# First-stage stores moved to GpSimd's queue, raw matrices loaded in thirds, and the statistics' roots unpinned, in a fused ConvNeXt block and gate

## The chip, the cores and the metric

The kernel runs on one core of a Trainium2 chip. The metric is the device time of one execution in microseconds (us). TensorE (PE) multiplies matrices and writes PSUM; VectorE (DVE), ScalarE (ACT) and GpSimd (POOL) do elementwise work; SyncE (SP) issues DMAs. Every engine works through its own instructions in order, and semaphores tie the engines together.

## The reference, cut to what matters

Thirty-two images of 384 channels, 28 x 28 pixels, go through a ConvNeXt block and then through a channel gate, all in float32:

```
y = depthwise_conv_7x7(x) + dw_b
y = (y - mean_c(y)) * rsqrt(var_c(y) + 1e-6) * ln_g + ln_b      # over channels, per pixel
y = gelu(y @ w1 + b1)                                           # 384 -> 1536
gx = sqrt(sum over pixels of y^2);  nx = gx / (mean_f(gx) + 1e-6)
y = grn_g * (y * nx) + grn_b + y
z = x + y @ w2 + b2                                             # 1536 -> 384
out = sigmoid(z + gate(mean, max, min of z over pixels))
```

## The kernel before

There are two parts. The **first stage** (lines 360 to 865) does the depthwise convolution of all images at once, channel by channel, as products on TensorE. The **image stage** (lines 869 to 1248) then takes the images one after the other: `up` (the product with w1), `down` (the product with w2), `gate_store`. Both matrix products are cut into block products with fewer multiplications (`UPSTEPS`, `STEPS`), which need sums of blocks of w1 and of w2. These sums (u1 and u2) are formed once, in the first stage, and kept in DRAM (`u1d`, `u2d`).

The first stage runs over 48 steps `s` of 8 channels each. A step has four pairs of channels. For a pair, `conv` (line 651) does six products into a PSUM tile `pc`; DVE transposes it into `yt` (line 682) and adds it to `acc` (line 690); ACT squares it into `sq` (line 696); after every second pair GpSimd adds `sq` to `ssum` (line 702). At the end of a step `yt` is stored to `yd` in DRAM (line 837). There are two `yt` buffers, two `sq` buffers and four `pc` buffers. Loads run ahead: the Toeplitz tables `tmat` (line 422) three steps, and the input planes (line 457) eight groups; a plane's buffer is free again when ACT has copied it into `xpad` (line 474), from where TensorE turns it (line 484) and DVE and ACT copy it into `xt` (lines 493, 495).

Between these lie the weights. `later` (line 633) says at which step a raw matrix or vector is loaded: w1 at step 2 and, into the same tile `ws`, w2 at step `U2 - 3` = 20. Ahead of each such load GpSimd writes one element of its target with a value of `acc` (line 788), so that the load waits for one engine only. `center_w` (line 561) folds the layer norm into w1 in steps 7 to 10: twelve groups of small products first, then twelve products into `pm`, and after every fourth of these three updates of w1 on DVE (line 597). `form_w` (line 543) makes one u tile: a first ACT or GpSimd instruction (lines 553, 550) and then one GpSimd addition for each further term (line 556). The fifteen u1 tiles are formed at the ends of steps 11 to 19, the thirty-eight u2 tiles at the ends of steps 23 to 44. All share three buffers of one tile (pool `ufp`). A finished tile is put into `stores` and stored by SP at the end of the next step (line 853).

The last two steps are done in two halves of sixteen images (line 802). Each half's `yt` is stored in quarters, by SP and ACT in turn (line 815). Then `finish` (line 711) makes the layer norm's statistics of a half on DVE, with a square root on ACT (line 730), and SP stores them (line 733) for the image stage, which reads them back as `rb` (line 289). `first_image` (line 748) prepares image 0 without the scale by its statistics, which `stretch` (line 904) multiplies in later. `normed` (line 308, operation on line 315) applies `rb` to the other images. In `up`, products go to PSUM banks `ph_A`, `ph_B`, `ph_C` (line 941), and each bank is evacuated by ACT copies (line 948) and DVE additions (lines 952 to 960).

What sets the order: the program is traced in the order of the code. The framework then places each instruction on its engine's list when its operands are ready, the earlier traced one first. `keep(...)`, or `tc.keep_in_program_order`, pins an instruction behind the one traced before it on its engine; without it an instruction may move ahead.

Of the kernel before, what the change touches and what calls it, by code (L numbers as in the profile page):

```python
# [23 lines left out]
EPS = 1e-6  # L24
# [9 lines left out]
TC = 8  # L34
# [12 lines left out]
SQ = 4  # L47
NQD = P // PW
# [40 lines left out]
KT = FB // 3  # L89
# [94 lines left out]
UD = 2  # L184
# [13 lines left out]
def convnext_gate_kernel(  # L198
# [109 lines left out]
    def normed(b, cbs=range(CB)):  # L308

        if b not in accs:  # L310
            accs[b] = (
                xp.tile([P, CB, NT], F32, tag="x", name=f"acc_{b}") if b == 1 else room_acc
            )
        for cb in cbs:
            nc.vector.scalar_tensor_tensor(  # L315
                accs[b][:, cb].rearrange("p (r w) -> p r w", w=HW), rows(yis[b][:, cb]),
                dwb_t[:, cb : cb + 1], rows(rbs[b]), ALU.add, ALU.mult,
            )

    def affine(eng, out, in_, mul, add):  # L320
        if eng is nc.vector:
# [38 lines left out]
    with ExitStack() as one:  # L360
# [78 lines left out]
        xi_last = tp.tile([P, NT], F32, name="xi_last")  # L439
        ssum = finp.tile([P, SQ, N], F32, name="ssum")  # L440
        acc = finp.tile([P, 2, N], F32, name="acc")
        fin = finp.tile([P, 3, N], F32, name="fin")
        dws = finp.tile([P, 1], F32, name="dws")
        lr = tp.tile([P, CB, 2], F32, name="lr")
        mcol = tp.tile([P, FB], F32, name="mcol")
        for t in (ssum, acc, fin[:, 0]):
            nc.gpsimd.memset(t, 0.0)
        GT = NX * NG
        xis = {}
# [15 lines left out]

        keep = tc.keep_in_program_order

        def pad_x(i):
            dst = xpad[i % NPAD][:, :, :HW]
            src = xis.pop(i).rearrange("p (r w) -> p r w", w=HW)  # L470
            if i < NG:
                nc.gpsimd.tensor_copy(dst, src)
            else:
                keep(nc.scalar.activation(dst, src, AF.Identity))

# [25 lines left out]
        w1r = ws.rearrange("p (k f) -> p k f", f=FF)  # L501
        w1v = ws.rearrange("p (k t m c) -> p t k m c", t=KT, m=3, c=P)
        w2v = ws.rearrange("p (t k m c) -> p t k m c", t=KD, k=4, c=P)
        U1, U2 = 11, 23
        stores = []
        SG = 20

# [32 lines left out]
                )  # L540


        def form_w(name, wv, text, dst):

            t = ufp.tile([P, KT, P], F32, tag="uf", name=name)[:, : wv.shape[1], :]
            todo = sorted(terms(text), key=lambda x: -x[0])
            blks = [(sg, wv[:, :, int(k), m, :]) for sg, m, k in todo]
            if len(blks) > 1 and blks[0][0] > 0:
                (_, a), (sg, c) = blks[:2]
                nc.gpsimd.tensor_tensor(t, a, c, ALU.add if sg > 0 else ALU.subtract)  # L550
                del blks[:2]
            else:
                keep(nc.scalar.activation(t, blks[0][1], AF.Identity, scale=float(blks[0][0])))
                del blks[:1]
            for sg, blk in blks:
                nc.gpsimd.tensor_tensor(t, t, blk, ALU.add if sg > 0 else ALU.subtract)
            stores.append((dst, t))

        cent = {}

# [43 lines left out]
        def pad_next(i):  # L604
            if i < GT:
                pad_x(i)
                if i + AHEAD < GT:
                    load_x(i + AHEAD)

        for i in range(AHEAD):  # L610
            load_x(i)
        xt = new_xt(0)
        for i in range(NG):
            pad_x(i)
            if i == 0:
                load_t(0, 2)
                nc.sync.dma_start(dwb, cvec[0:1, :].broadcast_to([P, C]))
            if i == NG - 2:
                for cb in range(CB):
                    if cb:  # L620
                        keep(sequences(cb))
                    keep(nc.scalar.dma_start(fs[cb][P:, :], zrow))
            if i == NG - 2:

                nc.gpsimd.tensor_copy(tmat[1][:, 0, :1], xpad[i % NPAD][:, 0, :1])
# [7 lines left out]
        later = {  # L633
            2: (
                ws.rearrange("p (cb f) -> p cb f", f=FF),
                w1.rearrange("(cb p) f -> p cb f", p=P),
            ),
            U2 - 3: (
                ws.rearrange("p (fb c) -> p fb c", c=C),
                w2.rearrange("(fb p) c -> p fb c", p=P),  # L640
            ),
            1: (cv, cvec.rearrange("v (cb p) -> p v cb", p=P)),
            4: (fv, fvec.rearrange("v (fb p) -> p v fb", p=P)),
            6: (awt[:, 0], aw[0].rearrange("(cb p) r -> p cb r", p=P)),
            7: (awt[:, 1], aw[1].rearrange("(cb p) r -> p cb r", p=P)),
            8: (w22b, w22.broadcast_to([P, R])),
# [61 lines left out]

        pcs = []

        def finish(half, b0, b1):

            def part(v):
                return v.rearrange("p (j b) -> p j b", b=B)[:, :, b0:b1]

            rs, s2 = (part(fin[:, i]) for i in range(2))
            mu, va = (part(acc[:, i]) for i in range(2))
            keep(nc.vector.tensor_tensor(mu, mu, va, ALU.add))
            keep(
                nc.vector.tensor_reduce(  # L720
                    s2,
                    ssum.rearrange("p c (j b) -> p j b c", b=B)[:, :, b0:b1],
                    AX.X, ALU.add,
                )
            )
            keep(nc.vector.tensor_scalar(mu, mu, dws, 1.0 / C, ALU.add, ALU.mult))
            keep(nc.vector.tensor_tensor(va, mu, mu, ALU.mult))
            keep(nc.vector.scalar_tensor_tensor(va, s2, 1.0 / C, va, ALU.mult, ALU.subtract))
            keep(nc.vector.tensor_scalar(va, va, 0.0, EPS, ALU.max, ALU.add))
            nc.scalar.activation(s2, va, AF.Sqrt)  # L730
# [44 lines left out]
        for s in range(NK):  # L775
            k, si = divmod(s, SK)
            if s + 3 < NK:
                if s == 0:
                    for i in range(2, 4):
                        nc.gpsimd.tensor_copy(tmat[i][:, 0, :1], xpad[i % NPAD][:, 0, :1])  # L780
                        if i == 2:
                            load_t(i)
                load_t(s + 3)
# [11 lines left out]
            if s == NK - 1:  # L795
# [6 lines left out]
                for half, (b0, b1) in enumerate(((0, B0), (B0, B))):  # L802
                    if b0 == b1:
                        continue
                    if half:
                        y2 = new_yt("yt_b0"), new_yt("yt_b1")
                        for i in range(0, NS, UG):
                            for t in range(2):
                                first_u1[t, i] = load_u1(t, i)
                    for n in range(2 * PAIRS):  # L810
                        i, c2 = divmod(n, PAIRS)
                        conv(NK - 2 + i, c2, y2[i], xt, b0, b1)
                        if c2 == PAIRS - 1:
                            for q in range(NQD):
                                (nc.sync, nc.scalar)[q % 2].dma_start(
                                    yd[
                                        q * B + b0 : q * B + b1,
                                        (NK - 2 + i) * TC : (NK - 1 + i) * TC, :,
                                    ],
                                    y2[i][q * B + b0 : q * B + b1],  # L820
                                )
# [6 lines left out]
            elif s < NK - 2:  # L828
                for c2 in range(PAIRS):
                    conv(s, c2, yt, xt, 0, B)  # L830
                    q = (s - U1 + 4) * PAIRS + c2
                    if 0 <= q < 4 * PAIRS:
                        for n in range(q * 3 // 2, (q + 1) * 3 // 2):
                            center_w(n)
                    if k + 1 < NX:
                        spread(k + 1, si * PAIRS + c2, xn)
                nc.sync.dma_start(yd[:, s * TC : (s + 1) * TC, :], yt)
# [81 lines left out]
    def up(b, hooks):  # L919
# [6 lines left out]
        for t2 in range(0, KT, 2):  # L926
            for i, (opnd, _, bk, first, acts) in enumerate(UPSTEPS):
                for t in (t2, t2 + 1):
# [359 lines left out]
```

## Time and profile before

| | |
|---|---|
| median of 3 runs | 3088.34 us (3086.13 to 3089.08) |
| the profiled execution | 3089.71 us |
| its span | 3087.7 us |
| mean granted TensorE clock | 0.993 of full |
| busy, of the span: PE, DVE, ACT, POOL | 98%, 65%, 59%, 79% |
| DMA: moved, mean rate | 673.24 MB, 218 GB/s |
| yd stores, first to last issue | 34.0 to 522.2 us, 46 of 896 KB |
| first products of image 0 (line 941) | 543.2 us |

The first stage takes the first 540 us or so. The page's line of DMA issues gives for the yd stores 6.3 us from issue to landing (median), for the w1 and w2 loads 12.8 us, for the u1 stores 6.7 and for the u2 stores 4.5.

How to read the parts shown below. A row of the table of windows has the stretch in us from the span's start, its length, then for each engine the busy time in it and the number of instructions, then the mean granted clock of TensorE, the busy share of the 16 DMA engines and the rate. A row of the waits names the engine and line that waited, what it waited for, and the total, the number and the longest of the waits. A row of the timeline has start, duration, engine, line, operation, output and input with their shapes, and in square brackets the idle time ahead of it and what ended it.

### The profile page before, as it was taken

Reading aid. Unit: us, or ns where it says so; the run is one execution under the profiler, and the core shown is the slowest. Engines: PE = TensorE matmul, PEld = TensorE weight load, DVE = VectorE, ACT = ScalarE, POOL = GpSimd, SP = SyncE. Lnnn points to the kernel's source line nnn. Section 1 sums busy time; section 2 is a strip of 40 time slices with the busy share of each in tenths; the row PEclk is TensorE's granted clock in tenths of the full one; section 3 lists DMA queues with packets and bytes.
Section 4 is the critical chain, followed back from the end, with each engine's and each line's share of the span. In section 5 each row is a group of like instructions: output and inputs, shape, how many; then the busy total and the mean of one; then the engine's idle time right before and its main releaser. Section 6 shows DMA issues by size and latency. Waiting matters only on the chain.

```text
span 3087.7 us, 44113 instructions
## 1 busy us (share of the span) xinstructions
PE 3011.4 (98%) x14435; PEld 2434.4 (79%) x14435; DVE 1994.1 (65%) x4554; ACT 1808.4 (59%) x3004; POOL 2438.7 (79%) x1829
## 2 busy tenths in 40 slices
PE   7999989889999999999999999999999999999998
PEld 7999989467777777777777777777777777777777
DVE  4565546766666666666666666666666666666666
ACT  3454555556666666666666666666666666666661
POOL 3365857389888888888888888888888888888897
PEclk9999999999999999999999999999999999999999
DMA  9799988555666666666666666666666666666546
GB/s 367 263 333 356 335 324 264 174 165 188 202 199 196 200 198 200 198 197 200 199 199 200 199 200 202 200 203 200 202 201 202 199 200 201 201 201 202 194 153 201
DMA packets 288476, 673.24 MB, mean 218 GB/s; under 512 B 31199, under 2 KB 111610, under 8 KB 282234
## 3 DMA queue, kind: packets, MB, share of 16 engines
q1 hardware_dynamic: 275156, 631.62, 62.2%
q10 hardware_dynamic: 13094, 38.80, 3.3%
q8 instruction: 118, 1.93, 0.3%
q14 instruction: 108, 0.88, 0.1%
HBM read 575.57 MB, written 94.76 MB: 217 GB/s over the span
## 4 chain that ended last, share of the span: by engine, by line
PE 86%; DVE 5%; POOL 4%; DMA 2%; ACT 1%; issue 1%; SPq 0%; DVEq 0%; ACTq 0%; POOLq 0%
PE ph_C L941 14%; PE ph_A L941 12%; PE ph_B L941 11%; PE pz_A L1071 8%; PE pz_C L1071 8%; PE pz_F L1071 7%; PE pz_D L1071 7%; PE pc L675 4%; PE pc L679 3%; PE pc L677 3%; PE pz_H L1071 2%; PE pz_I L1071 2%; PE pz_E L1071 2%; PE pt L484 2%; DVE room L315 2%
## 5 line engine op out<-in xcount | busy, mean ns | idle before, releaser
L324 ACT ACTIVATE y<-y,fv,gsc 128x784 f32<-128x784 f32 x372 | 359.1, 1031 | 464.8 <-DVE gsc L979 464.8
L1032 POOL TENSOR_TENSOR d_room<-y 128x588 f32<-128x588 f32 x253 | 364.4, 1442 | 289.6 <-PE pz_B L1071 192.2
L941 PE MATMUL ph_C<-room,ws 128*128 128x392 f32 x1240 | 464.6, 497 | 9.1 <-DVE y L952 3.8
L900 ACT ACTIVATE y<-y,b1f 128x784 f32<-128x784 f32 x384 | 349.9, 944 | 200.9 <-DVE y L958 179.0
L941 PE MATMUL ph_B<-room,ws 128*128 128x392 f32 x1240 | 459.6, 493 | 6.8 <-ACT y L948 4.3
L941 PE MATMUL ph_A<-room,ws 128*128 128x392 f32 x1240 | 458.8, 492 | 2.0 <-POOL room L356 2.0
L1032 POOL TENSOR_TENSOR d_room<-d_room,y 128x588 f32<-128x588 f32 x308 | 440.7, 1435 | 16.8
L941 PEld LDWEIGHTS ph_C<-room,ws 128*128 128x128 f32 x1240 | 234.0, 191 | 193.8 <-DVE y L956 28.5
L941 PEld LDWEIGHTS ph_A<-room,ws 128*128 128x128 f32 x1240 | 235.8, 190 | 175.6 <-POOL room L356 2.7
L941 PEld LDWEIGHTS ph_B<-room,ws 128*128 128x128 f32 x1240 | 234.7, 190 | 171.2 <-ACT y L948 5.0
L702 POOL TENSOR_TENSOR ssum<-ssum,sq 128x896 f32<-128x896 f32 (+1 forms) x100 | 201.5, 2015 | 184.2 <-ACT sq L696 183.8
L913 ACT ACTIVATE junk<-y 128x784 f32<-128x784 f32 x384 | 329.0, 857 | 9.0
L1032 POOL TENSOR_TENSOR d_room<-y,d_room 128x588 f32<-128x588 f32 x214 | 306.0, 1436 | 26.9 <-PE pz_D L1071 15.8
L356 POOL TENSOR_TENSOR room<-room 128x392 f32<-128x392 f32 x303 | 303.4, 1018 | 11.9
L696 ACT ACTIVATE sq<-pc,dwb 128x224 f32<-128x224 f32 x368 | 144.5, 444 | 227.0 <-DVE acc L690 211.4
L1032 POOL TENSOR_TENSOR y<-y 128x588 f32<-128x588 f32 x180 | 258.6, 1437 | 7.1
L682 DVE STREAM_TRANSPOSE yt<-pc 128x448 f32<-128x448 f32 x184 | 119.5, 649 | 208.3 <-PE pc L679 194.9
L954 DVE TENSOR_TENSOR y<-y,ph_B 128x392 f32<-128x392 f32 x256 | 137.2, 556 | 155.2 <-ACT y L900 123.5
L952 DVE TENSOR_TENSOR y<-y,ph_C 128x392 f32<-128x392 f32 x384 | 212.4, 561 | 25.2
L675 PE MATMUL pc<-xt,tmat 128*128 128x224 f32 x736 | 203.2, 358 | 2.6 <-ACT xt L495 2.6
L1071 PE MATMUL pz_A<-d_room,u 128*128 128x196 f32 x1050 | 202.9, 329 | 0.1
L1071 PEld LDWEIGHTS pz_A<-d_room,u 128*128 128x128 f32 x1050 | 178.8, 190 | 7.7 <-POOL d_room L1032 0.4
(265 smaller groups left out, 6374.6 us busy)
## 6 DMA issues: line engine op xcount, KB each, us to landing
u<-u2d SPq DMA_DIRECT2D x487, 384.0 KB, 3.8
ws<-u1d SPq DMA_DIRECT2D x384, 320.0 KB, 3.0
tmat<-fs SPq DMA_DIRECT2D x47, 1420.0 KB, 8.8
ws<-u2d SPq DMA_DIRECT2D x121, 384.0 KB, 3.8
yi<-yd SPq DMA_DIRECT2D x95, 448.0 KB, 6.3
yd<-yt SPq DMA_DIRECT2D x46, 896.0 KB, 6.3
x<-in_x SPq DMA_DIRECT2D x32, 1176.0 KB, 5.5
out<-x ACTq DMA_DIRECT2D x31, 1176.0 KB, 9.2
```

Source lines behind the costliest of these rows:

```text
L324: eng.activation(out, in_, AF.Identity, bias=add, scale=mul)
L356: tc.keep_in_program_order(eng.tensor_tensor(d, o[in0], o[in1], op))
L675: keep(nc.tensor.matmul(po, t[:, c, P : 2 * P], xc, start=True, stop=False))
L696: nc.scalar.activation(part(sq)[:, cy % SQ + ci], part(pc[:, :, :N])[:, ci], AF.Square, bias=dwb[:, cc + ci : cc + ci + 1], scale=1.0,)
L702: nc.gpsimd.tensor_tensor(part(ssum), part(ssum), part(sq), ALU.add)
L900: ins = nc.scalar.activation(y, y, AF.Gelu, bias=b1f[:, f : f + 1], scale=1.0)
L913: ins = nc.scalar.activation(junk, ys[b][:, f, :], AF.Square, accum_out=ssqs[b][:, f : f + 1])
L941: nc.tensor.matmul(banks[t, bk][:, :NH], wts[t][:, i % UG, :], o[opnd], start=(first == 1), stop=True, skip_group_check=True,)
L952: nc.vector.tensor_tensor(d, d, p, ALU.add)
L954: nc.vector.tensor_tensor(d, d, p, ALU.subtract)
L1032: nc.gpsimd.tensor_tensor(d[0], o[a][0], o[c][0], ALU.add if sign == "+" else ALU.subtract)
L1071: nc.tensor.matmul(pz[:, :NQ4], wt[:, i % UD, t, :], o[opnd][0][:, t, :], start=(first and t == 0), stop=(t == KD - 1), skip_group_check=True,
```

## The change

- The yd stores of steps 0 to 45 and all u stores are issued on GpSimd's queue, pinned: a yd store behind the step's last `ssum`, the u stores behind the yd store.
- w1 is loaded in three DMAs at steps 3, 4, 5, and w2 in three at steps 21, 22, 23. The vector pack `fv` comes at step 2 instead of 4.
- `U1` and `U2` are 12 and 24: u1 tiles are formed in steps 12 to 20, u2 tiles in steps 24 to 44.
- A u2 tile is half of a buffer, and each pair is stored in one DMA of 384 KB; there are three such buffers. u1 tiles take a buffer each.
- In `center_w`'s second part four products are made at once, three pairs of channels apart.
- In the first half of the last two steps, `yt` is stored whole by SP; the second half is stored in quarters as before.
- `finish` is no longer pinned, and its tile `fin` comes from the pool of `sq`.
- In `up`, the ACT copies of image 0 are pinned only in its second half (`t2` = 2). `normed` of image 1 is pinned.
- The copies of the first planes into `xpad` on GpSimd are pinned, and the markers ahead of the loads of `tmat` 2 and 3 read one and the same `xpad`.

```diff
@@ normed
-            nc.vector.scalar_tensor_tensor(
+            ins = nc.vector.scalar_tensor_tensor(
...
+            if b == 1:
+                tc.keep_in_program_order(ins)
@@ first stage
-        fin = finp.tile([P, 3, N], F32, name="fin")
...
             if i < NG:
-                nc.gpsimd.tensor_copy(dst, src)
+                keep(nc.gpsimd.tensor_copy(dst, src))
...
-        U1, U2 = 11, 23
+        U1, U2 = 12, 24
@@ form_w
-        def form_w(name, wv, text, dst):
-
-            t = ufp.tile([P, KT, P], F32, tag="uf", name=name)[:, : wv.shape[1], :]
+        pair = {}
+
+        def form_w(name, wv, text, to, dst=()):
+
+            if not dst or dst[0] == 0:
+                pair["t"] = ufp.tile([P, UD * KD, P], F32, tag="uf", name=name)
+            n = wv.shape[1]
+            at = dst[0] * n if dst else 0
+            t = pair["t"][:, at : at + n, :]
...
-            stores.append((dst, t))
+            if not dst:
+                stores.append((to, t))
+            elif dst[0] == UD - 1:
+                stores.append((to, pair["t"]))
@@ markers of tmat
+        def hold(dst, i):
+            nc.gpsimd.tensor_copy(dst, xpad[i % NPAD][: dst.shape[0], 0, :1])
...
-                        nc.gpsimd.tensor_copy(tmat[i][:, 0, :1], xpad[i % NPAD][:, 0, :1])
+                        hold(tmat[i][:, 0, :1], NG)
@@ later
-            2: (
-                ws.rearrange("p (cb f) -> p cb f", f=FF),
-                w1.rearrange("(cb p) f -> p cb f", p=P),
-            ),
...
+            **{
+                3 + cb: (
+                    ws.rearrange("p (cb f) -> p cb f", f=FF)[:, cb],
+                    w1[cb * P : (cb + 1) * P, :],
+                )
+                for cb in range(CB)
+            },
+            **{
+                U2 - 3 + i: (
+                    ws.rearrange("p (fb c) -> p fb c", c=C)[:, 4 * i : 4 * i + 4],
+                    w2[4 * i * P : (4 * i + 4) * P, :].rearrange("(fb p) c -> p fb c", p=P),
+                )
+                for i in range(3)
+            },
@@ finish
+            if not half:
+                fins.append(sqp.tile([P, SQ, N], F32, tag="sq", name="fin"))
+                nc.vector.memset(fins[0][:, 0], 0.0)
+            fin = fins[0]
...
-            keep(nc.vector.tensor_tensor(mu, mu, va, ALU.add))
+            (nc.vector.tensor_tensor(mu, mu, va, ALU.add))
...
             nc.scalar.activation(s2, va, AF.Sqrt)
-            keep(nc.vector.reciprocal(rs, s2))
-            keep(nc.vector.transpose(fin[:, 2], fin[:, 0]))
+            (nc.vector.reciprocal(rs, s2))
+            (nc.vector.transpose(fin[:, 2], fin[:, 0]))
@@ last two steps
+                            ch = slice((NK - 2 + i) * TC, (NK - 1 + i) * TC)
+                            if not half:
+                                nc.sync.dma_start(yd[:, ch, :], y2[i])
+                            else:
+                                for q in range(NQD):
...
@@ a step
-                    q = (s - U1 + 4) * PAIRS + c2
-                    if 0 <= q < 4 * PAIRS:
+                    q = (s - U1 + 5) * PAIRS + c2
+                    if 0 <= q < 2 * PAIRS:
                         for n in range(q * 3 // 2, (q + 1) * 3 // 2):
                             center_w(n)
+                    elif q in (2 * PAIRS + 2, 2 * PAIRS + 5, 2 * PAIRS + 8):
+                        n = FB + 4 * ((q - 2 * PAIRS) // 3)
+                        for i in range(4):
+                            center_w(n + i)
...
-                nc.sync.dma_start(yd[:, s * TC : (s + 1) * TC, :], yt)
+                keep(nc.gpsimd.dma_start(yd[:, s * TC : (s + 1) * TC, :], yt))
...
             for dst, u in stores:
-                nc.sync.dma_start(dst, u)
+                keep(nc.gpsimd.dma_start(dst, u))
...
-                    u2d[i // UD].rearrange("p (u t c) -> p u t c", u=UD, c=P)[:, i % UD],
+                    u2d[i // UD].rearrange("p (u c) -> p u c", c=P), (i % UD,),
@@ up
-                            if b < 2:
+                            if b == 1 or (b == 0 and t2):
                                 tc.keep_in_program_order(ins)
```

More of the change, by code (lines that the diff above doesn't have):

```diff
@@ L445, in convnext_gate_kernel @@
         mcol = tp.tile([P, FB], F32, name="mcol")
-        for t in (ssum, acc, fin[:, 0]):
+        for t in (ssum, acc):
             nc.gpsimd.memset(t, 0.0)
@@ L466, in convnext_gate_kernel @@
         keep = tc.keep_in_program_order
+        keep = tc.keep_in_program_order
         def pad_x(i):
             dst = xpad[i % NPAD][:, :, :HW]
-            src = xis.pop(i).rearrange("p (r w) -> p r w", w=HW)
+            src = xis[i].rearrange("p (r w) -> p r w", w=HW)
             if i < NG:
-                nc.gpsimd.tensor_copy(dst, src)
+                keep(nc.gpsimd.tensor_copy(dst, src))
             else:
@@ L623, in convnext_gate_kernel @@
             if i == NG - 2:
-                nc.gpsimd.tensor_copy(tmat[1][:, 0, :1], xpad[i % NPAD][:, 0, :1])
+                hold(tmat[1][:, 0, :1], i)
                 load_t(1)
@@ L633, in convnext_gate_kernel @@
         later = {
-            2: (
-                ws.rearrange("p (cb f) -> p cb f", f=FF),
-                w1.rearrange("(cb p) f -> p cb f", p=P),
-            ),
[L638 to L641, printed above, removed]
+            **{
[12 more added lines that the diff above has]
+            },
             1: (cv, cvec.rearrange("v (cb p) -> p v cb", p=P)),
-            4: (fv, fvec.rearrange("v (fb p) -> p v fb", p=P)),
+            2: (fv, fvec.rearrange("v (fb p) -> p v fb", p=P)),
             6: (awt[:, 0], aw[0].rearrange("(cb p) r -> p cb r", p=P)),
@@ L709, in convnext_gate_kernel @@
         pcs = []
+        fins = []
         def finish(half, b0, b1):
+            if not half:
+                fins.append(sqp.tile([P, SQ, N], F32, tag="sq", name="fin"))
+                nc.vector.memset(fins[0][:, 0], 0.0)
+            fin = fins[0]
             def part(v):
@@ L717, in finish @@
             mu, va = (part(acc[:, i]) for i in range(2))
-            keep(nc.vector.tensor_tensor(mu, mu, va, ALU.add))
-            keep(
+            (nc.vector.tensor_tensor(mu, mu, va, ALU.add))
+            (
                 nc.vector.tensor_reduce(
@@ L725, in finish @@
             )
[L726 to L729, printed above, removed]
+            (nc.vector.tensor_scalar(mu, mu, dws, 1.0 / C, ALU.add, ALU.mult))
+            (nc.vector.tensor_tensor(va, mu, mu, ALU.mult))
+            (nc.vector.scalar_tensor_tensor(va, s2, 1.0 / C, va, ALU.mult, ALU.subtract))
+            (nc.vector.tensor_scalar(va, va, 0.0, EPS, ALU.max, ALU.add))
             nc.scalar.activation(s2, va, AF.Sqrt)
-            keep(nc.vector.reciprocal(rs, s2))
-            keep(nc.vector.transpose(fin[:, 2], fin[:, 0]))
+            (nc.vector.reciprocal(rs, s2))
+            (nc.vector.transpose(fin[:, 2], fin[:, 0]))
             nc.sync.dma_start(rsd[half], fin[:, 2])
@@ L813, in convnext_gate_kernel @@
                         if c2 == PAIRS - 1:
[L814 to L821, printed above, removed]
+                            ch = slice((NK - 2 + i) * TC, (NK - 1 + i) * TC)
[3 more added lines that the diff above has]
+                                for q in range(NQD):
+                                    (nc.sync, nc.scalar)[q % 2].dma_start(
+                                        yd[q * B + b0 : q * B + b1, ch, :],
+                                        y2[i][q * B + b0 : q * B + b1],
+                                    )
                     if not half:
```

## The prediction

> **What bounds the kernel now.** I read the granted clock and the page first, then the busy times by stretch, then the waits of the first 560 us, then single stretches of the timeline. The stretches, from the table of windows:
>
> ```profile
> core 0: us, PE busy (x) PEld busy (x) DVE busy (x) ACT busy (x) POOL busy (x), PEclk, DMA share, GB/s
> 65.00:78.00 13.00, 6.67 (x28) 5.93 (x27) 4.61 (x8) 3.33 (x7) 2.08 (x1) 0.74 1.03 403
> ...
> 136.00:152.00 16.00, 12.21 (x70) 11.46 (x69) 8.63 (x15) 5.57 (x13) 4.17 (x2) 0.89 0.71 264
> ...
> 248.00:256.00 8.00, 5.07 (x25) 4.54 (x24) 3.50 (x6) 3.33 (x7) 7.47 (x6) 0.79 1.03 365
> ...
> 307.00:318.00 11.00, 7.59 (x40) 6.93 (x39) 3.60 (x6) 6.73 (x17) 6.13 (x4) 0.84 0.87 318
> 318.00:417.00 99.00, 98.30 (x618) 94.19 (x617) 57.74 (x99) 55.20 (x124) 79.07 (x58) 1.00 0.95 346
> 417.00:433.00 16.00, 7.22 (x28) 6.68 (x28) 3.00 (x5) 4.38 (x10) 2.08 (x1) 0.68 0.78 272
> ...
> 545.00:565.00 20.00, 11.78 (x25) 6.07 (x26) 12.63 (x29) 2.91 (x8) 0.00 (x0) 0.84 0.77 255
> ...
> 630.00:3080.00 2450.00, 2432.52 (x11056) 1911.22 (x11055) 1627.85 (x3907) 1484.04 (x2298) 2093.76 (x1577) 1.00 0.61 198
> ```
>
> After 630 us TensorE is busy 99% at full clock, so what the first stage loses or gains arrives one to one at the end. Inside the first stage TensorE is also the bound, except in a few holes. Idle time is length less PE busy, and a clock of 0.74 over 13 us loses another 0.26 x 13. So the holes cost: 65:78 6.3 + 3.4 = 9.7 us; 136:152 3.8 + 1.8 = 5.6; 248:256 2.9 + 1.7 = 4.6; 307:318 3.4 + 1.8 = 5.2; 417:433 8.8 + 5.1 = 13.9; together **39.0 us**. The handover, 545:565, costs 8.2 + 3.2 = 11.4. Their causes, from the waits of the first 560 us (total, times, longest):
>
> ```profile
> DVE yt L682 <- DMA yd<-yt: 13.4, 4, 7.2
> ...
> POOL u L550 <- DMA u2d<-u: 11.5, 3, 6.2
> ...
> ACT fin L730 <- DVE acc L729: 9.3, 2, 5.9
> ACT u L553 <- DMA u2d<-u: 9.2, 1, 9.2
> ...
> ACT u L553 <- DMA yd<-yt: 7.3, 1, 7.3
> ...
> PE pm L588 <- DVE ws L597: 3.8, 2, 3.1
> ...
> DVE acc L690 <- POOL ws L788: 2.8, 1, 2.8
> ```
>
> The 7.2 us is the hole at 65: a yd store issued at 52.6 behind the 2304 KB load of w1 (49.9) lands 16.1 us later. The 7.3 and 9.2 us on ACT are the holes at 307 and 417: L553 wants a u buffer whose store has just been issued, and all of ACT queues behind it. L588 is the hole at 136. The 2.8 us is the hole at 248: the marker copy that opens w2's load (L788) stands behind u formation on GpSimd, and DVE may not overwrite acc before it.
>
> **What the skill says.** (1) "TensorE: Matmul & The Clock Gate", Part 1: after about 3.4 us of little activity the clock halves until a busy window has passed. The trace agrees: 0.68 to 0.84 in the holes of 2.9 us and up, 1.00 in 318:417. (2) "DMA: Bandwidth & Descriptors", Queues, rings and completion order: each DMA engine takes turns between the rings of different issuers, but works in order within one. The 16.1 us landing fits the second half; no run here shows the first. (3) Same page, SWDGE vs HWDGE vs iDMA: a DMA issued by GpSimd has its descriptors written by GpSimd's own cores; by its Specifications the first byte takes about 1 us, against 0.6. The trace has only hardware queues, so this is the unknown. (4) "SBUF — State Buffer", Who interferes with whom: two-port DVE modes lock GpSimd out. The frequent DVE operations of this stage (L682, L690, L493) read PSUM, so I price this at nothing.
>
> **The change part by part.**
>
> *yd stores on GpSimd's queue (46).* Removed from SP's queue: the wait of the store behind loads that are not ready (SP waits on xpad for 187 us in total). Added: each issue occupies GpSimd for a time g that this trace doesn't show. SP spends 0.54 us (median of L837) on the same issue; the skill's first byte is 1 us. I take g = 1.0; ends 0.3 and 2.6. It waits for DVE's last transpose, which is over before the ssum ahead of it starts, so the wait itself is free; queued behind it are the u stores, the u additions and the next ssum, for which ACT's sq waits. Pinned behind that ssum, the store starts later than now. One step:
>
> ```profile
> 402.93 0.65 DVE L682 STREAM_TRANSPOSE yt<-pc 128x448 f32<-128x448 f32 x1 [0.74 <-PE pc L679]
> 403.89 0.54 SPq L837 DMA_DIRECT2D yd<-yt  x1
> 405.11 2.09 POOL L702 TENSOR_TENSOR ssum<-ssum,sq 128x896 f32<-128x896 f32 x1 [2.86 <-ACT sq L696]
> 414.31 0.65 DVE L682 STREAM_TRANSPOSE yt<-pc 128x448 f32<-128x448 f32 x1 [0.90 <-PE pc L679]
> ```
>
> The last transpose of a step starts at 402.93; its ssum ends at 407.20, 4.3 us later; with two yt buffers the store must have landed by 414.31, 11.4 us after 402.93. Four successive steps give 11.4, 12.6, 12.6 and 12.9, mean 12.4. So 4.3 + g + L must stay under 12.4, where L is the landing (median 6.2 now, 4.0 to 16.1). With its own ring the 896 KB should get half of the 374 GB/s moved in the first 65 us, 4.8 us, and 1 to 2 us around it: L = 6.5. Sum 11.8: it fits, with 0.6 us to spare. The hole at 65 goes: **-9.7**.
>
> *w1 and w2 in thirds at three steps each.* Same bytes; 768 KB instead of 2304 KB stand ahead of other transfers. Markers: four more of 0.18 us. Nothing on the path except the first w2 marker, below. The loads have three to four steps' lead to hide in.
>
> *u2 in pairs, three buffers of two.* At two u forms a step a third of three single buffers waits for a store just issued; with six places the store has a whole step. Holes at 307 and 417: **-5.2 and -13.9**. At 417 SP's y loads also stood ahead of the store, and no longer do. The u1 tiles still have three buffers, so their waits (4.8 us, three times) stay.
>
> *Row-mean products three pairs apart.* Each group's DVE updates (3 x 0.66 us) have 7 us: the hole at 136 goes, **-5.6**.
>
> *u a step later.* First w2 marker: it now stands behind ssum, the yd store, two u1 stores and a first u addition (1.3 us): 4.3 + 3g + 1.3 = 8.6 us after the start of a step's last transpose, where it was at 248.8 - 243.5 = 5.3. acc on DVE waits for it, ACT's sq for acc. The hole at 248 grows: **+3** (ends -5, all hidden, and +8).
>
> *GpSimd's load.* It is the cover for everything above:
>
> ```profile
> core 0: us, POOL busy (x), PEclk, DMA share, GB/s
> ...
> 309.00:386.00 77.00, 65.19 (x50) 0.98 0.93 335
> ```
>
> It is 85% busy here. In the new order steps 26 to 31 form eleven u2 tiles, 32 additions of 1.02 us; two ssum of 2.08 a step make 25.0; 1.9 stores a step make 11.4 g. Sum 69 us at g = 1, in six steps of 9.9 us = 59.4: 9.6 us over, of which ssum's two sq buffers and PSUM hide some 4 (at 307 a stall of ACT of 7.3 left a hole of 3.4). I charge 6, plus 1 for steps 37 and 38 and 2 for step 19's six u1 additions of 1.3 us: **+9** (ends: 3 at g = 0.5, 30 at g = 2).
>
> *End of the stage.* The last yd store before the halves goes at 522.2 from SP; on GpSimd it follows five u additions and two ssum that end at 525.0, and yt_a (3.3 us of waiting already) waits on: **+3**. One 896 KB store instead of four of 112 KB: 448 KB more to move, about 1 us, against two issues fewer on ACT: nothing net.
>
> *Roots, copies, normed.* ACT stands 5.9 and 3.4 us at the roots (L730) with evacuations behind; DVE stands 5.2 us at L315 (561.3) for rb with two evacuations behind. Unpinned copies and a pinned normed(1) free both. But DVE is late next: from 542.4 it has 4.7 us of forms, 8 of statistics, 13 of evacuations (22 x 0.6) and 3 of normed, 29 us, that end at 571 where TensorE ended this half at 575.5. I take **-5**; ends +3 and -11 (the whole of 545:565).
>
> *At nothing:* fin in sq's pool (it waits for an ssum that ends by 541, before the roots), fv two steps earlier (18 KB), the second marker of tmat on another xpad (that load has 30 us of lead), the pads pinned at the start (their order is that of their data).
>
> Sum: -9.7 - 5.2 - 13.9 - 5.6 + 3 + 9 + 3 - 5 = -24.4. The profiled execution took 3089.7 us, span 3087.7 and 2.0 around it: 3065.3. The median of the runs is 1.4 lower, so I forecast **3064**.
>
> **The rivals.** *The store loop binds (slower).* If g + L exceeds 8.1, each of 46 steps grows by the excess: DVE waits at L682 for the buffer, TensorE for DVE. Without the +9, which this replaces, the gain is 33; at 0.7 us a step (g + L = 8.8) it is used up, and at 9.1 the time is 3088 - 33 + 46 = 3101. For: landings of 16 us occur, and DMA is 95% busy in the best stretches. Against: half the bandwidth gives 6.5. *The stalls move to GpSimd.* g near 1.5: the load costs 17 instead of 9, the marker 5 more and half-clock windows 3 more: 3080. For: 85% busy already. *Everything is absorbed.* g near 0.3, load 0, marker free (-4.6 instead of +3), yt_a +1, handover -8: 3064 - 9 - 7.6 - 2 - 3 = 3042. *The unpinned part does nothing*, since an unpinned instruction may be placed where it was: forecast + 5, inside the first case.
>
> **How the numbers follow.** Forecast 0.52, GpSimd stalls 0.14, all absorbed 0.14, slower 0.20. About 0.2%, 6 us, is what can be told from no change. Faster: 0.52 + 0.14 + 0.14 less 0.02 of the second's tail = 0.78; same: that 0.02 and 0.03 of the store loop just past its threshold; slower: its other 0.17. Range 3042 to 3094: it leaves out 0.06 below and 0.12 above.
>
> **What would show it.** Right: no DVE wait on yd stores over 3 us; no L553 or L550 wait on u2 stores; PE busy over 98% from 60 to 240 and 260 to 500; GpSimd's DMA issues near 1 us. Wrong: L682 waiting for yd a little in every step, step length over 10.3 us; ACT's sq waiting for ssum by tens of us; a hole over 8 us at the w2 marker.

## The result and the profile after

The changed kernel takes 3117.12 us (median of four runs, 3109.92 to 3120.50), the kernel before on the same chip 3088.71 (3086.13 to 3091.51). The ratio is **1.0089 [1.0067, 1.0111]**: some 28 us slower, where 24 us less was forecast. The profiled execution took 3120.5 us, its span is 3118.8.

The table of windows of the changed kernel, for its holes (columns as before: stretch, length, busy times, granted clock, DMA share, rate):

```profile
60.00:190.00 130.00, 127.35 (x824) 122.47 (x823) 76.60 (x134) 63.45 (x142) 57.70 (x46) 0.99 0.88 327
199.00:213.00 14.00, 6.60 (x25) 6.08 (x25) 4.66 (x8) 4.54 (x10) 9.45 (x7) 0.63 0.71 268
265.00:281.00 16.00, 6.38 (x26) 5.72 (x25) 6.05 (x11) 5.56 (x13) 12.74 (x12) 0.68 0.60 199
344.00:358.00 14.00, 7.29 (x33) 6.59 (x32) 4.66 (x8) 3.85 (x9) 8.61 (x8) 0.76 0.70 270
388.00:410.00 22.00, 13.38 (x63) 12.33 (x63) 9.61 (x17) 8.27 (x20) 16.80 (x14) 0.84 0.59 216
444.00:458.00 14.00, 8.89 (x43) 8.11 (x42) 5.30 (x10) 4.50 (x10) 3.96 (x4) 0.76 0.71 266
550.00:570.00 20.00, 10.19 (x77) 9.86 (x76) 5.89 (x14) 4.67 (x16) 10.38 (x11) 0.74 0.68 244
570.00:590.00 20.00, 15.33 (x77) 10.60 (x76) 17.86 (x41) 7.63 (x21) 4.53 (x4) 0.83 0.67 166
670.00:3110.00 2440.00, 2423.45 (x11025) 1906.12 (x11023) 1619.03 (x3889) 1475.73 (x2280) 2082.47 (x1569) 1.00 0.60 198
```

Priced as in the prediction (idle time plus the missing share of the clock), the five holes from 199 to 458 cost 12.6 + 14.7 + 10.1 + 12.1 + 8.5 = 58.0 us and the last two steps with the handover, from 550 to 590, another 23.1, together 81.1. Before, the same sum was 39.0 + 11.4 = 50.4. The difference, 30.7, is that of the two profiled executions (3120.5 - 3089.7 = 30.8), so on balance little is lost elsewhere. The first row holds the gain: the holes at 65 and 136 are gone. It also holds a small new loss, 4.1 us in steps 7 and 8 (counted from 0; 92 to 123 us), in which DVE waits 10.3 us for a load of the gate's weights. The rest of the new loss lies after 190 us, where u tiles are formed, and at the end of the stage.

The waits of the first 590 us of the changed kernel (total, times, longest):

```profile
DVE yt L703 <- DMA yd<-yt: 59.0, 14, 8.3
ACT sq L717 <- POOL ssum L723: 27.3, 8, 5.6
POOL u L559 <- DMA u2d<-u: 27.3, 5, 8.0
POOL u L559 <- DMA u1d<-u: 12.2, 4, 4.9
DVE yt_a L703 <- DMA yd<-yt: 12.2, 1, 12.2
ACT u L562 <- DMA u1d<-u: 6.6, 2, 5.8
DVE acc L711 <- POOL ws L816: 5.5, 1, 5.5
ACT fin L758 <- DVE acc L757: 3.7, 1, 3.7
```

Of the kernel before (first 560 us), the waits for these that the prediction doesn't show as lines:

```profile
ACT sq L696 <- POOL ssum L702: 8.8, 6, 1.9
...
POOL u L550 <- DMA u1d<-u: 4.8, 3, 2.9
...
DVE yt_a L682 <- DMA yd<-yt: 3.3, 1, 3.3
```

DVE waits for yd stores by 59.0 us (13.4 before), ACT for `ssum` by 27.3 (8.8), GpSimd for u1 and u2 stores by 39.5 (16.3). The roots (L758, formerly L730) wait less, 3.7 against 9.3.

What happens in one hole is seen on GpSimd's timeline of the changed kernel:

```profile
334.30 1.02 POOL L559 TENSOR_TENSOR u<-ws 128x384 f32<-128x384 f32 x1 [4.48 <-DMA u2d<-u]
335.40 2.08 POOL L565 TENSOR_TENSOR u<-u,ws 128x384 f32<-128x384 f32 x2
337.44 2.08 POOL L723 TENSOR_TENSOR ssum<-ssum,sq 128x896 f32<-128x896 f32 x1
339.47 0.56 POOL L870 DMA_DIRECT2D yd<-yt  x1
340.02 0.55 POOL L886 DMA_DIRECT2D u2d<-u  x1
340.58 2.10 POOL L723 TENSOR_TENSOR ssum<-ssum,sq 128x896 f32<-128x896 f32 x1
349.37 1.02 POOL L559 TENSOR_TENSOR u<-ws 128x384 f32<-128x384 f32 x1 [6.69 <-DMA u2d<-u]
350.33 2.10 POOL L723 TENSOR_TENSOR ssum<-ssum,sq 128x896 f32<-128x896 f32 x1
352.37 0.56 POOL L870 DMA_DIRECT2D yd<-yt  x1
```

and on DVE's:

```profile
339.76 0.65 DVE L703 STREAM_TRANSPOSE yt<-pc 128x448 f32<-128x448 f32 x1 [0.90 <-PE pc L700]
...
348.46 0.65 DVE L703 STREAM_TRANSPOSE yt<-pc 128x448 f32<-128x448 f32 x1 [7.54 <-DMA yd<-yt]
```

DVE finishes a step's `yt` with the transpose at 339.76. Its store should follow some 4 us later. But ahead of it in GpSimd's list stands the addition of 349.37, which wants a u buffer whose store GpSimd itself issued at 340.02; it waits 6.69 us. The `ssum` and the yd store queued behind go at 350.33 and 352.37, 12.6 us after the transpose. This store still lands before DVE needs its buffer again. The hole comes from the step before, which had the same: its store was issued at 339.47 instead of about 334, behind an addition that waited 4.48 us, and landed at 348.36. So DVE stands for 7.54 us until 348.46, and TensorE, which waits for `xpad` from ACT, as ACT waits for DVE, is idle from 344.6 to 351.3. That nothing overtakes the waiting addition is what the Trainium skill says in "PSUM — Partial Sum Buffer", Engine vs sequencer instructions: GpSimd's queue is strict FIFO; the rows above agree.

### The profile page after: what moved, and what is told of

It reads as the page before. It is cut to its first block, busy times and chain, and to the rows that moved or that the text cites. A ratio compares the mean times of both kernels' runs of the same rounds, so it can differ in the third digit from the quotient of the medians.

```text
span 3118.8 us, 44072 instructions
## 1 busy us (share of the span) xinstructions
PE 3019.9 (97%) x14435; PEld 2441.6 (78%) x14435; DVE 1992.4 (64%) x4555; ACT 1808.0 (58%) x3004; POOL 2484.5 (80%) x1912
## 4 chain that ended last, share of the span: by engine, by line
PE 79%; POOL 7%; DMA 5%; DVE 4%; issue 2%; ACT 2%; ACTq 0%; DVEq 0%; SPq 0%; POOLq 0%
PE ph_C L974 13%; PE ph_A L974 12%; PE ph_B L974 11%; PE pz_C L1104 7%; PE pz_A L1104 7%; PE pz_D L1104 7%; PE pz_F L1104 7%; PE pc L696 2%; PE pz_H L1104 2%; PE pz_I L1104 2%; PE pz_E L1104 2%; PE pc L700 2%; PE pc L698 2%; POOL d_room L1065 2%; DVE room L315 2%
```

## The experiments

**Theory** (place in the list): a yd store on GpSimd stands behind every u addition traced before it, with that addition's wait, and comes late; and the additions wait for u stores that are issued late in the same list. **Rivals**: issue work (80 issues fill GpSimd); one ring (u stores land behind 896 KB of yd); the longer landing of a GpSimd store by itself; pairs (a pair buffer is held too long); another part of the change. The ratios compare each kernel with the kernel before on the same chip; absolute times of the experiments come from three chips.

### The yd stores back on SP

```diff
-                keep(nc.gpsimd.dma_start(yd[:, s * TC : (s + 1) * TC, :], yt))
+                nc.sync.dma_start(yd[:, s * TC : (s + 1) * TC, :], yt)
```

> The changed kernel with the yd stores back on SP's queue, unpinned; the u stores stay on GpSimd. Coupling (GpSimd waits for a u buffer and the yd store, queued behind that wait, comes late): most of the loss goes, 3070 to 3085 us against 3117, and DVE's waits for yt fall from 59 us to under 20 while GpSimd's waits for u buffers stay. Issue cost (46 issues of 0.57 us fill GpSimd): up to 26 us come back too, but then GpSimd's waits for u buffers, which are the end of a backlog, change as well. Pairs (a pair buffer is held for too long): 3105 or more, since the waits for u buffers go on holding ssum and with it ACT.

Measured: 3096.43 us, ratio 1.0010 [1.0001, 1.0018]. Less came back than the theory of a mere coupling asked for. DVE's wait for `yt` fell to 20.1 us, but GpSimd's own waits stayed, and with them ACT's for `ssum` (57.5 us). GpSimd's timeline of this kernel shows the circle bare:

```profile
320.80 0.57 POOL L886 DMA_DIRECT2D u2d<-u  x1
332.03 1.02 POOL L559 TENSOR_TENSOR u<-ws 128x384 f32<-128x384 f32 x1 [10.66 <-DMA u2d<-u]
```

The store is issued, and the next instruction in the same list waits 10.66 us for it to land. It is the slowest landing of a u2 store in this kernel, 11.2 us; the median is 6.4.

### The u stores back on SP

```diff
-                keep(nc.gpsimd.dma_start(dst, u))
+                nc.sync.dma_start(dst, u)
```

> The changed kernel with the u stores back on SP's queue, unpinned; the yd stores stay pinned on GpSimd. Coupling: the yd stores still stand behind every wait for a u buffer, so the time stays over 3095 us unless the waits themselves vanish. One ring for both kinds of store (u lands late behind 896 KB of yd): the u stores land in some 5 us instead of 7.5, the waits for u buffers fall by half, and the time falls to 3080 to 3095. Issue cost: 34 issues of 0.6 us come back, about 3100.

Measured: 3095.61 us, 1.0004 [0.9997, 1.0012]. GpSimd waits for no u store at all now; yet eight yd stores are issued more than 6 us after their last transpose, and DVE waits for yd stores by 52.4 us. So it isn't only waits that delay a store. GpSimd's timeline of this kernel:

```profile
230.28 2.55 POOL L559 TENSOR_TENSOR u<-ws 128x512 f32<-128x512 f32 x2
232.80 2.49 POOL L565 TENSOR_TENSOR u<-u,ws 128x512 f32<-128x512 f32 x2
235.25 2.09 POOL L723 TENSOR_TENSOR ssum<-ssum,sq 128x896 f32<-128x896 f32 x1
237.31 2.60 POOL L565 TENSOR_TENSOR u<-u,ws 128x512 f32<-128x512 f32 x2
239.87 1.30 POOL L559 TENSOR_TENSOR u<-ws 128x512 f32<-128x512 f32 x1
241.24 1.28 POOL L565 TENSOR_TENSOR u<-u,ws 128x512 f32<-128x512 f32 x1
242.47 1.29 POOL L559 TENSOR_TENSOR u<-ws 128x512 f32<-128x512 f32 x1
243.85 2.62 POOL L565 TENSOR_TENSOR u<-u,ws 128x512 f32<-128x512 f32 x2
246.43 2.08 POOL L723 TENSOR_TENSOR ssum<-ssum,sq 128x896 f32<-128x896 f32 x1
248.46 0.58 POOL L870 DMA_DIRECT2D yd<-yt  x1
```

Eleven additions traced before the store stand ahead of it, with one `ssum` between. The `yt` was complete at 235.5, when seven of them were still to come; the store goes at 248.46, and DVE waits 10.65 us for it, until 258.59.

### Both back on SP

```diff
-                keep(nc.gpsimd.dma_start(yd[:, s * TC : (s + 1) * TC, :], yt))
+                nc.sync.dma_start(yd[:, s * TC : (s + 1) * TC, :], yt)
...
-                keep(nc.gpsimd.dma_start(dst, u))
+                nc.sync.dma_start(dst, u)
```

> The changed kernel with all stores back on SP's queue, unpinned: what remains of the change are thirds, pairs a step later, spaced pm products, unpinned finish and copies. Coupling, issue cost and one ring all expect 3055 to 3080 us, under the kernel before. Another part as the cause (pairs, unpinned finish, the whole store at the half): over 3095 us.

Measured: 3060.92 us, 0.9890 [0.9876, 0.9904]. The rest of the change is worth 33 us. GpSimd's timeline of this kernel, same place:

```profile
232.13 1.30 POOL L559 TENSOR_TENSOR u<-ws 128x512 f32<-128x512 f32 x1
233.51 1.27 POOL L565 TENSOR_TENSOR u<-u,ws 128x512 f32<-128x512 f32 x1
234.91 2.08 POOL L723 TENSOR_TENSOR ssum<-ssum,sq 128x896 f32<-128x896 f32 x1
238.02 1.29 POOL L559 TENSOR_TENSOR u<-ws 128x512 f32<-128x512 f32 x1 [1.03 <-DMA u1d<-u]
239.38 1.28 POOL L565 TENSOR_TENSOR u<-u,ws 128x512 f32<-128x512 f32 x1
240.62 2.09 POOL L723 TENSOR_TENSOR ssum<-ssum,sq 128x896 f32<-128x896 f32 x1
```

With no yd store on GpSimd the additions lie between the `ssum`, two at a time. Against this kernel the yd stores on GpSimd add 1.14% (35 us), the u stores 1.20% (37 us), both 1.99% (61 us); they share some holes. Each kind costs more than half of this when it has GpSimd's ring to itself, so a shared ring is not needed for the loss.

### The queue alone, in the kernel before

```diff
-                nc.sync.dma_start(yd[:, s * TC : (s + 1) * TC, :], yt)
+                keep(nc.gpsimd.dma_start(yd[:, s * TC : (s + 1) * TC, :], yt))
...
-                nc.sync.dma_start(dst, u)
+                keep(nc.gpsimd.dma_start(dst, u))
```

> The kernel before with nothing changed but the queue: yd and u stores on GpSimd, pinned as in the changed kernel. Coupling: slower, 3100 to 3130 us, with DVE waits for yt of 30 us or more, though u tiles are single. Pairs as the cause: 3075 to 3090, no more DVE waiting than before (13.4 us). Issue cost: 3095 to 3105, spread over all steps with u forms.

Measured: 3143.18 us, 1.0162 [1.0145, 1.0179]: +50 us with single u tiles, more than anything that was expected, DVE's wait for `yt` 39.1 us, and ACT's at L553 for u2 stores 53.6. Pairs are not the cause; without them it is no better.

### Both on GpSimd, not pinned

```diff
-                keep(nc.gpsimd.dma_start(yd[:, s * TC : (s + 1) * TC, :], yt))
+                nc.gpsimd.dma_start(yd[:, s * TC : (s + 1) * TC, :], yt)
...
-                keep(nc.gpsimd.dma_start(dst, u))
+                nc.gpsimd.dma_start(dst, u)
```

> The changed kernel with both kinds of store still on GpSimd, but not pinned: the framework may put each where its data are ready. Place in the list (a pinned store stands behind the step's second ssum and every u addition traced before it, and the u additions behind it wait for a store in the same list): a good part of the loss goes, 3065 to 3095 us against 3117. Issue work (80 issues of 0.55 to 0.77 us fill GpSimd): nothing is taken away, so it stays at 3105 to 3120.

Measured: 3088.49 us, 0.9981 [0.9973, 0.9990]. The same 80 issues, and a little over half of the 61 us is back (33 us). The yd stores now go ahead of the second `ssum`, a u store right behind its tile, and GpSimd's wait for u2 stores is 3.1 us. Five yd stores are still issued over 6 us after their last transpose, and the 28 us that remain against the kernel with both on SP are not taken apart.

### Each u store right behind its own tile

The loop over `stores` is moved behind the calls of `form_w`; all stores stay pinned on GpSimd.

```diff
-            for dst, u in stores:
-                keep(nc.gpsimd.dma_start(dst, u))
-            stores.clear()
             for i in range(NS):
...
                     u2d[i // UD].rearrange("p (u c) -> p u c", c=P), (i % UD,),
                 )
+            for dst, u in stores:
+                keep(nc.gpsimd.dma_start(dst, u))
+            stores.clear()
```

> The changed kernel with each u store issued on GpSimd right behind the last addition of its own tile, instead of a step later; yd stores unchanged. Place in the list: the buffers come free earlier, GpSimd's waits for u buffers (about 40 us with longest 8) fall under 15 us and the time falls towards that of the kernel with the u stores on SP's queue, 3092 to 3102 us. Issue work: the same number of issues, 3110 to 3120.

Measured: 3103.80 us, 1.0036 [1.0024, 1.0049]; GpSimd's waits for u stores are 12.9 us, not 39.5. So 0.53%, 16 us, of the loss came from issuing u stores a step later behind other work.

### Occupancy without a transfer

Both stores on SP, and in the place of the yd store:

```diff
+                for _ in range(3):
+                    keep(nc.gpsimd.memset(junk, 0.0))
```

> All stores on SP's queue, and on GpSimd, pinned behind each step's last ssum, three memsets of one element, some 0.17 us each by the marker copies, in the place of the yd store's 0.57 us issue: the occupancy and the pinned place, but no transfer that anyone waits for. Issue work: most of the 35 us that the yd stores cost on GpSimd comes, 3080 to 3095 us. Place in the list (what costs is that DVE waits for a store that comes late): 3060 to 3067, as the kernel with all stores on SP's queue (3061).

Measured: 3063.39 us, 0.9903 [0.9888, 0.9918]: as without them (0.9890). The three memsets take 0.41 us, less than I had put down, but 0.7 of an issue. So much work at this place costs nothing; with the unpinned stores above, which keep all 80 issues, issue work as the main cause falls. A late place alone costs nothing either: in six steps the last memset runs over 6 us after the last transpose (up to 9.4), but nothing waits for it. GpSimd's timeline of this kernel, in step 19, the step shown above for the u stores on SP:

```profile
242.65 0.10 POOL L873 MEMSET junk<- 128x1 f32 x1
242.70 1.28 POOL L566 TENSOR_TENSOR u<-u,ws 128x512 f32<-128x512 f32 x1
243.91 0.27 POOL L873 MEMSET junk<- 128x1 f32 x2
244.14 1.28 POOL L566 TENSOR_TENSOR u<-u,ws 128x512 f32<-128x512 f32 x1
```

Between the step's last transpose and its last memset run three additions, where seven ran ahead of the store. So the pin by itself does not explain how many additions stand ahead of the store in this step; what else does is not shown.

### Fewer additions ahead of the store

The kernel with only the yd stores on GpSimd, with all further additions of the u tiles (L565) left out; its u tiles hold only their first one or two terms.

```diff
-            for sg, blk in blks:
-                nc.gpsimd.tensor_tensor(t, t, blk, ALU.add if sg > 0 else ALU.subtract)
```

> The kernel with the yd stores pinned on GpSimd and the u stores on SP's queue, with GpSimd's further additions of the u tiles (66 instructions of about 1 us, L565) left out, so that the u tiles hold only their first one or two terms. Place in the list (the additions stand ahead of the pinned store): the late yd stores of steps 19, 23 and 28 go, and the time falls from 1.0004 of the kernel before to 0.988 or less, some 3050 to 3060 us. If a store on GpSimd's queue costs by its landing (7.7 us median there against 6.8 on SP's), the holes stay: 3080 us or more.

Measured: 3065.91 us, 0.9920 [0.9908, 0.9932]: 26 of 35 us are back, though the landing stays long (7.9 us median). Four yd stores, not eight, are issued over 6 us after their last transpose; those of steps 19, 23 and 28, which were expected to go, are among them. The miss of some 12 us against the 0.988 expected is mostly one hole, at 294, of which GpSimd's timeline of this kernel shows the cause:

```profile
279.53 4.90 POOL L559 TENSOR_TENSOR u<-ws 128x384 f32<-128x384 f32 x5 [6.89 <-DMA ws<-in_w]
284.38 2.09 POOL L721 TENSOR_TENSOR ssum<-ssum,sq 128x896 f32<-128x896 f32 x1
286.41 0.58 POOL L868 DMA_DIRECT2D yd<-yt  x1
```

The first u2 additions wait 6.89 us for w2's load, and again a yd store stands behind them, 14.0 us after its last transpose (272.39). It is the same mechanism with another wait.

### A version that beats both: only the first twelve yd stores on GpSimd

```diff
+                if s < U1:
+                    keep(nc.gpsimd.dma_start(yd[:, s * TC : (s + 1) * TC, :], yt))
+                else:
+                    nc.sync.dma_start(yd[:, s * TC : (s + 1) * TC, :], yt)
```

> All stores on SP's queue except the yd stores of steps 0 to 11, ahead of the first u tile, which stay pinned on GpSimd. Both theories expect that these twelve cost nothing, since GpSimd is a third to half busy there; the hole at 65 us goes that the kernel with all stores on SP's queue still has: 3052 to 3060 us against its 3061. If the issue or the longer landing cost something by themselves in each step: 3063 or more.

Measured: 3057.10 us, **0.9880 [0.9867, 0.9894]**. Where no u tile is formed, a store on GpSimd costs nothing that can be told. In the table of windows, first of the kernel with both on SP, then of this one:

```profile
60.00:80.00 20.00, 14.56 (x81) 13.67 (x80) 7.75 (x15) 6.88 (x18) 6.45 (x5) 0.83 0.98 339
```

```profile
60.00:190.00 130.00, 127.10 (x822) 122.24 (x820) 76.56 (x133) 64.36 (x143) 60.96 (x46) 0.99 0.91 331
190.00:500.00 310.00, 307.20 (x1954) 294.73 (x1953) 181.59 (x320) 173.92 (x394) 223.47 (x156) 1.00 0.95 348
```

The hole at 66 (5.4 us idle, 20 us at clock 0.83) is filled, and from 190 to 500 TensorE is busy for 99% at full clock. The step times of the two traces differ by 3.7 us at the end of the stage; the ratios' intervals overlap.

### Three parts undone in that version

The pins of `finish` and of image 0's copies back, and `normed` unpinned:

```diff
-            (nc.vector.tensor_tensor(mu, mu, va, ALU.add))
+            keep(nc.vector.tensor_tensor(mu, mu, va, ALU.add))
...
-                            if b == 1 or (b == 0 and t2):
+                            if b < 2:
```

> The version with all stores on SP's queue but the first twelve yd stores, with one part undone: finish and the ACT copies of image 0 pinned as before, normed of image 1 unpinned. If the freed evacuations are worth what the stretch between the last step and the second image shows (7 us less in the kernel with all stores on SP's queue): 3062 to 3067 us against 3057. If an unpinned instruction stays where it was: 3057.

Measured: 3055.40 us, 0.9889 [0.9875, 0.9902]: no difference that can be told. The u2 tiles single:

```diff
-                pair["t"] = ufp.tile([P, UD * KD, P], F32, tag="uf", name=name)
...
+            t = ufp.tile([P, KT, P], F32, tag="uf", name=name)[:, : wv.shape[1], :]
```

> The same version with u2 tiles single again, in three buffers of one tile, a step later than in the kernel before. If the pairs took away the holes at 307 and 417 us: 3069 to 3078 us against 3057, with ACT or GpSimd waiting for u2 stores by 15 us or more. If the place of the forms did it (a step later): 3057 to 3062.

Measured: 3070.26 us, 0.9937 [0.9924, 0.9949], 18 us by the ratios; ACT waits for u2 stores by 34.2 us and GpSimd by 22.7. The raw matrices whole:

```diff
+            3: (
+                ws.rearrange("p (cb f) -> p cb f", f=FF),
+                w1.rearrange("(cb p) f -> p cb f", p=P),
+            ),
+            U2 - 3: (
+                ws.rearrange("p (fb c) -> p fb c", c=C),
+                w2.rearrange("(fb p) c -> p fb c", p=P),
+            ),
```

> The same version with w1 and w2 loaded whole again, w1 at step 3 and w2 at step 21. If the thirds matter only where a store stands behind the load on SP's queue, w1's no longer does (the first yd stores are on GpSimd's), and only w2's can cost: 3057 to 3064 us against 3057. If the thirds gave the 4 us at step 21: at the upper end of this.

Measured: 3054.33 us, 0.9884 [0.9869, 0.9899]: no difference. By the step times the early steps win 3.4 us and steps 23 and 24 lose 2.0; neither can be put down to the loads, since the early steps of two kernels with thirds (this version and that with single tiles) differ by 4.7.

### What the runs say together

From the traces, the time from the start of a step's last transpose to the issue of its yd store, over 46 steps:

| kernel | median us | over 6 us | longest | ratio |
|---|---|---|---|---|
| before (SP) | 0.96 | 1 | 8.5 | 1 |
| before, all stores on GpSimd | 4.22 | 15 | 19.0 | 1.0162 |
| changed (GpSimd, pinned) | 4.21 | 14 | 18.6 | 1.0089 |
| u stores right behind their tiles | 4.22 | 11 | 20.6 | 1.0036 |
| yd stores on SP | 1.12 | 2 | 9.9 | 1.0010 |
| u stores on SP | 4.21 | 8 | 14.8 | 1.0004 |
| both unpinned | 0.95 | 5 | 16.9 | 0.9981 |
| few additions, u stores on SP | 4.21 | 4 | 14.0 | 0.9920 |
| both on SP | 0.97 | 2 | 10.0 | 0.9890 |
| first twelve on GpSimd | 3.43 | 0 | 4.2 | 0.9880 |

The median says nothing about the time. Among the kernels whose yd stores all go through GpSimd, the fewer are late, the faster the kernel. The row with the yd stores on SP is the other half of the cause: few stores are late, and it is slow all the same, since GpSimd's additions wait 45.4 us for u stores and ACT behind them for `ssum`.

## Why the prediction was wrong, by its steps

- **The yd store's price: this step failed.** It said that the store "waits for DVE's last transpose, which is over before the ssum ahead of it starts, so the wait itself is free", and listed what is queued *behind* the store. What is queued *ahead* of it was counted as one `ssum`. In the steps without u tiles that is right: 4.2 us, and 4.2 + a landing of 6.8 us, 11.0, stays under the loop's 12.4. In the others up to nine additions (twelve with the u stores on SP), and waits of 3 to 8 us, stand ahead, and the store goes up to 18.6 us after the last transpose. With the yd stores alone that costs 35 us. Of the prediction's signs of being wrong two came: ACT waits 27.3 us for `ssum`, and the hole at the w2 marker costs 14.7.
- **g and L.** Taken 1.0 and 6.5; measured 0.57 and 6.8. The store loop, my slower rival, was not what made it slower. Nothing shows GpSimd held up by DVE, priced at nothing: `ssum` takes 2.09 us in both kernels.
- **GpSimd's load, +9: wrong in kind.** It was priced as throughput (69 us of work in 59 us). The memsets show that 0.41 us more in each step was free; both queue moves cost 61 us, of which 33 come back when the same issues, unpinned, stand elsewhere in the list. My rival "the stalls move to GpSimd" named the engine, but made it depend on g near 1.5; at 0.57 it happened all the same.
- **Pairs, -5.2 and -13.9: right for a store on SP**, where steps 25 and 26 together gain 5.0 us and step 36 gains 11.6, and undoing the pairs costs 18. On GpSimd the claim that "the store has a whole step" fails: the store goes behind other work, lands after 7.5 us, and L559 waits 27.3 us for u2. The u1 waits didn't stay at 4.8 either but grew to 12.2 on GpSimd and 6.6 on ACT.
- **Hole at 136, -5.6, and at 65, -9.7: right in the mechanism.** In the changed kernel step 4 gains 8.8 us and steps 9 to 11 gain 5.7; the latter do so with both on SP too. Steps 7 and 8 lose 4.1, and by step 12 it is 9.7 us ahead, less than the sum of 15.3.
- **w2 marker, +3: the wait is right** (L711 waits 5.5 us, 2.8 before), the list ahead of it too short: the copy runs at 271.28, 16.5 us after the last transpose and not 8.6. Behind the first addition, where it was expected, come another `ssum`, four more additions, a u1 store and a wait of 3.65 us for a u1 store. The hole around it costs 14.7 us, but not by the marker alone: DVE waits before that until 265.31 for the yd store of step 19, issued 12.4 us after its last transpose and landed at 265.22.
- **End of the stage, +3: too small.** `yt_a` waits 12.2 us for the last yd store, 9 more than before; with both on SP 2.6.
- **Roots, copies, normed, -5: no measurable value** by their own run. The wait at L758 shrank, without saving time. From image 0's first products to that of its `grn` (`pg`, line 971 of the kernel before) it takes 76.4 us before, 72.9 with both on SP, 71.6 with the first twelve on GpSimd, and still 72.4 with the pins back; which part does that stays open.
- **Thirds at nothing:** right where no yd store stands behind w1. Whole loads with all stores on SP were not tried.

Without the queue terms the sum of the prediction (pairs -19.1, spacing -5.6, roots -5) is -29.7; the kernel with both on SP measures -33. So close a match is partly chance: the roots' -5 could not be measured, and step 20 gains 4.3 us there, where the marker was charged +3. But the error, in sign and most of its size, is the queue: 61 us lie between that kernel and the changed one.

Two readings of the prediction need a word. The clock in the five holes is 0.68 to 0.89, not to 0.84 (136:152). The 374 GB/s are those of 20 to 65 us; the whole first 65 us have 358.

## What to carry to other kernels

Before moving a DMA to the queue of an engine that computes, write down what stands *ahead* of it in that engine's list in the busiest step, waits included, and not only its issue time and what it blocks: a list is no faster than its head. If the engine itself later waits for that DMA, the list can wait for itself. Here the pinned stores cost 33 us more than the unpinned ones. Where the engine has no such work, as in the first twelve steps, the move cost nothing that could be told.

## What the runs showed of the hardware

A GpSimd DMA issue occupied GpSimd for 0.57 us (896 KB), 0.55 (384 KB) and 0.76 (u1, 256 KB), about SP's 0.54 for the first; I had taken 1.0. The yd stores' landing from GpSimd's queue was 6.8 us (median) in the changed kernel and 6.0 to 9.2 in the other runs with all of them there; from SP's, in the landings that the traces hold, 6.3 before and 6.8 with both on SP. The Trainium skill's "DMA: Bandwidth & Descriptors", Anatomy of one DMA — SWDGE (gpsimd) path, fits 2.0 us plus bytes over 436,000 for each us; that is an estimate of 4.1 us for 896 KB. The shortest here took 3.8, most more beside the other transfers.
